# A decoder layer with experts: routed rows gathered in blocks, scores made by key, and an order planned in the source

## The chip, the cores and the metric

The kernel runs on one core of a Trainium2 chip. The metric is the device time of one execution in microseconds (us); the time of a kernel is the median over several runs. A profiled execution of each kernel gives the views that are quoted. The engines are PE (TensorE matmuls), PEld (its weight loads), DVE (VectorE), ACT (ScalarE), POOL (GpSimd) and SP (SyncE, which issues transfers here).

## The reference

One layer over 32 sequences of 128 tokens, width 128, 16 heads of width 8, all in fp32. Biases and gains are drawn at random, so none can be left out.

```
x, encoder_output: (32, 128, 128)     H, HD, FF, E, K = 16, 8, 512, 8, 2

def _attn(q_in, k_in, v_in, ..., causal):
    Q, Kp, V = q_in @ wq + bq, k_in @ wk + bk, v_in @ wv + bv      # by head
    scores = einsum('bqhd,bkhd->bhqk', Q, Kp) / sqrt(HD)           # -inf where causal and k > q
    a = softmax(scores)
    return einsum('bhqk,bkhd->bqhd', a, V) @ wo + bo

def _moe(x, ...):
    router_weights = softmax(x @ rw + rb)
    topw, topi = top_k(router_weights, 2);  topw = softmax(topw)
    combine[t, topi] += topw                                        # (tokens, 8)
    h = gelu(x @ w1[e] + b1[e]);  eo = h @ w2[e] + b2[e]            # every expert e
    return sum over e of eo[e] * combine[:, e]

x = layernorm(x + _attn(x, x, x, ..., True)) * g1 + b1
x = layernorm(x + _attn(x, encoder_output, encoder_output, ..., False)) * g2 + b2
x = layernorm(x + _moe(x)) * g3 + b3
```

## The kernel before, in words

Four sequences form a group (`G`), eight groups the input. The attention goes through groups: the loop at L409 runs the self attention of group `gi` and the cross attention of group `gi - 1` as two Python generators, one step of each in turn. There is no planner: each engine takes its instructions in the order in which the program writes them, and a tile pool makes an instruction wait until the buffer that it is to fill has been read.

In a group's attention, `transposed` (L200 to L205) turns the inputs on PE, ACT copies them out of PSUM. `keys_values` (L207 to L236) makes K under four head masks (`kb`) and V filled up with zeros to 32 columns a head. `probabilities` (L248 to L273) makes scores with a row for each query, eight heads at a time, in one of two PSUM pairs (`ps_sc`): where masked, first a bf16 product of the identity with the causal mask (L257), then two matmuls on tiles of 32 rows (L263). DVE takes each head's maximum (L268) and subtracts it (L269), and ACT takes the exponential (L272). `values` (L275 to L304) turns all 16 heads' probabilities on PE (L281), copies them out on ACT (L283), multiplies with V on column tiles of 128x32 (L285), turns the result back (L293) and divides it by its sum (L298, L299). Behind it come the output matmul (L320), the sum with the input (L322), and the norm: DVE's statistics (L174, L176), POOL's power (L177, L178), DVE's scaling (L180), POOL's gain and bias (L327, L328). `route` (L362 to L400) makes the router's logits, finds the two largest and leaves eight combine weights for each token, six of them zero.

The experts (L428 to L470) follow when all attention is done. For every group and every one of the eight experts, all 512 tokens go through: four matmuls of 512 columns (L448), four GELUs on ACT (L452), sixteen matmuls of 128 columns (L458), and four DVE steps that add the result times its combine weight (L463). Then the last norm and the store. Transfers: groups' inputs and results on SP's queue, experts' weights on POOL's (L404), all other weights on ACT's.

Of the kernel before, what the change touches and what calls it, by code (L numbers as in the profile page):

```python
# [9 lines left out]
BF16 = mybir.dt.bfloat16  # L10
U32 = mybir.dt.uint32
# [11 lines left out]
VC = 32  # columns of a column group of TensorE  # L23
RG = 4  # row groups of TensorE, of four heads each
EPS = 1e-05
SCALE = 1.0 / float(HD) ** 0.5
# Added to a masked score it leaves no bit of the score; exact in bfloat16.
MASKED = -(2.0**100)


def bc(ap, axis, n):
# [4 lines left out]
    return ap.broadcast_to(shape)  # L36


@with_exitstack
def kernel(  # L40
# [36 lines left out]
    NG = B // G  # L77

    const = ctx.enter_context(tc.tile_pool(name="const", bufs=1))
    keep = ctx.enter_context(tc.tile_pool(name="keep", bufs=1))  # L80

# [1 line left out]
    ident = const.tile([P, P], F32, name="ident")  # L83
    make_identity(nc, ident)
    ident16 = const.tile([P, P], BF16, name="ident16")
    nc.vector.tensor_copy(ident16, ident)

    # causal[q, r, k] = 0 where k <= q, else MASKED
    causal = const.tile([P, RG, P], BF16, name="causal")
    nc.gpsimd.memset(causal, 0.0)  # L90
    nc.gpsimd.affine_select(
        out=causal,
        in_=causal,
        pattern=[[0, RG], [-1, P]],
        compare_op=ALU.is_ge,
        fill=MASKED,
        base=0,
        channel_multiplier=1,
    )

    # hmask[p, r] = 1 where p lies in the head r of its row group: 0 <= p - 32 g - 8 r < 8 for a g
    hm4 = const.tile([P, RG, 4], F32, name="hm4")
    nc.gpsimd.memset(hm4, 1.0)
    nc.gpsimd.affine_select(
        out=hm4, in_=hm4, pattern=[[-32, RG], [-8, 4]], compare_op=ALU.is_ge,
        fill=0.0, base=0, channel_multiplier=1,
    )
    nc.gpsimd.affine_select(
# [59 lines left out]
    def normalize(y, name):  # L168
# [4 lines left out]
        for t in range(G):  # L173
            nc.vector.bn_stats(st[:, t, :], y[:, t, :])  # L174
# [337 lines left out]
```

## Time and profile before

| | before |
|---|---|
| median of 3 runs | 1370.74 us (1361.25 to 1379.28) |
| span of the profiled execution | 1358.0 us |
| PE busy | 1130.1 us (83%) |
| DVE busy | 549.3 us (40%) |
| ACT busy | 549.2 us (40%) |
| POOL busy | 146.6 us (11%) |
| attention, from the first to the last of its work on PE | 30.4 to 853 us |
| experts | 853 to 1347.5 us |

For the profiled execution the profile gives the span, from its first to its last record, and no time of its own beside it: the runs stand 3.25 to 21.28 us above that span. In the views, a group's row reads: line, engine, operation, out<-in, shapes, count, then busy us, mean ns of one, and the idle time ahead with what ended it. `128*32` is the tile of PE's array in use. A row of the windows reads: stretch, length, busy time and count for each engine, the clock granted to PE as a share of full speed, the share of time in which the DMA engines moved data, and GB/s.

### The profile page before, as it was taken

The page shows a single profiled execution, that of the slowest core. Times are in us where ns is not written, and L with a number is a line of the kernel's source. Part 1 is how long each engine was busy: PE and PEld are TensorE (multiplying, and loading weights), DVE is VectorE, ACT ScalarE, POOL GpSimd, SP SyncE. Part 2 cuts the span into 40 slices and gives each one's busy share as a digit, 9 for nine tenths or more (in the row PEclk, how much of TensorE's full clock was granted, in tenths as well). Part 3 has the DMA queues.
Part 4 walks back from the last instruction along what each step waited for, and adds up shares of the span by engine and source line. Part 5 has one row for each costly group of instructions (what it writes and reads, how often), then busy time and mean ns, then how long its engine had stood idle before and what let it go on. Part 6 is the DMA issues. An engine that isn't in the chain of part 4 may idle for free.

```text
span 1358.0 us, 17518 instructions
## 1 busy us (share of the span) xinstructions
PE 1130.1 (83%) x7196; PEld 697.2 (51%) x7233; DVE 549.3 (40%) x1286; ACT 549.2 (40%) x822; POOL 146.6 (11%) x173
## 2 busy tenths in 40 slices
PE   3969679579679858957957958799999999999996
PEld 1444344344344534543433433477777777776775
DVE  1548358266355356436636534222121221212121
ACT  1445345345343524524625623543333333343342
POOL 4020200300200020030030030101010110101011
PEclk9989879878975967778978975799999999999998
DMA  6000000000000000000000000000000000000000
GB/s 190 1 16 1 8 9 1 9 8 1 8 9 0 2 15 1 0 9 8 1 0 1 1 0 0 1 1 8 1 8 1 8 1 8 9 1 9 1 8 8
DMA packets 17551, 12.81 MB, mean 9 GB/s; under 512 B 1816, under 2 KB 16448, under 8 KB 17472
## 3 DMA queue, kind: packets, MB, share of 16 engines
q1 hardware_dynamic: 12672, 6.29, 1.6%
q0 software_dynamic: 1280, 4.20, 1.0%
q10 hardware_dynamic: 3520, 1.21, 0.4%
q8 instruction: 57, 0.93, 0.3%
q14 instruction: 22, 0.18, 0.0%
HBM read 9.60 MB, written 2.10 MB: 9 GB/s over the span
## 4 chain that ended last, share of the span: by engine, by line
PE 72%; DVE 12%; ACT 7%; POOL 4%; issue 3%; DMA 1%; ACTq 0%; POOLq 0%; DVEq 0%
PE po L458 17%; PE ph L448 17%; PE sc_s L263 7%; PE sc_c L263 5%; PE pt_c L281 5%; PE pt_s L281 4%; PE po_c L285 3%; PE po_s L285 3%; DVE nm_s L268 2%; DVE pr_s L269 2%; ACT prT_s L283 2%; PE pu_s L293 1%; POOL x L327 1%; POOL x L328 1%; PE sc_s L257 1%
## 5 line engine op out<-in xcount | busy, mean ns | idle before, releaser
L452 ACT ACTIVATE h<-ph,b1T 128x512 f32<-128x512 f32 x256 | 175.6, 687 | 291.2 <-PE ph L448 285.8
L458 PEld LDWEIGHTS po<-w,h 128*128 128x128 f32 x2048 | 247.9, 192 | 58.4 <-issue 43.5
L458 PE MATMUL po<-w,h 128*128 128x128 f32 x2048 | 250.1, 276 | 0.1
L448 PE MATMUL ph<-x2T,w 128*128 128x512 f32 x512 | 244.9, 600 | 0.0
L463 DVE SCALAR_TENSOR_TENSOR acc<-po,comb,acc 128x128 f32<-128x128 f32 x256 | 72.1, 344 | 359.2 <-PE po L458 359.2
L268 DVE TENSOR_REDUCE nm_s<-sc_s 128x8 f32<-128x1024 f32 x64 | 78.2, 1222 | 109.7 <-PE sc_s L263 109.7
L448 PEld LDWEIGHTS ph<-x2T,w 128*128 128x128 f32 x512 | 87.7, 192 | 62.3 <-issue 61.2
L263 PE MATMUL sc_s<-kb_s,q_s 32*128 32x512 f32 x256 | 107.7, 778 | 6.4 <-issue 2.3
L281 PE MATMUL pt_s<-ident,pr_s 128*128 128x128 f32 x512 | 87.8, 307 | 23.4 <-ACT pr_s L272 23.4
L268 DVE TENSOR_REDUCE nm_c<-sc_c 128x8 f32<-128x1024 f32 x64 | 77.9, 1217 | 60.9 <-PE sc_c L263 60.9
L283 ACT COPY prT_s<-pt_s 128x512 f32<-128x512 f32 x128 | 70.8, 586 | 69.8 <-PE pt_s L281 67.9
L283 ACT COPY prT_c<-pt_c 128x512 f32<-128x512 f32 x128 | 70.2, 588 | 69.1 <-PE pt_c L281 69.1
L272 ACT ACTIVATE pr_s<-pr_s 128x1024 f32<-128x1024 f32 x64 | 67.9, 1061 | 63.4 <-DVE pr_s L269 63.0
L281 PEld LDWEIGHTS pt_s<-ident,pr_s 128*128 128x128 f32 x512 | 62.0, 154 | 60.9 <-issue 34.6
L263 PE MATMUL sc_c<-kb_c,q_c 32*128 32x512 f32 x256 | 83.5, 764 | 8.2 <-DVE pr_s L269 4.8
L281 PE MATMUL pt_c<-ident,pr_c 128*128 128x128 f32 x512 | 88.5, 311 | 0.0
L272 ACT ACTIVATE pr_c<-pr_c 128x1024 f32<-128x1024 f32 x64 | 67.7, 1057 | 41.4 <-DVE pr_c L269 41.2
L204 PE MATMUL tp_x<-ident,x 128*128 128x128 f32 x64 | 16.1, 400 | 80.4 <-POOL x L328 78.5
L269 DVE TENSOR_TENSOR pr_c<-sc_c,nm_c 128x1024 f32<-128x1024 f32 x64 | 78.2, 1222 | 2.9
L269 DVE TENSOR_TENSOR pr_s<-sc_s,nm_s 128x1024 f32<-128x1024 f32 x64 | 77.6, 1212 | 1.0
L281 PEld LDWEIGHTS pt_c<-ident,pr_c 128*128 128x128 f32 x512 | 62.9, 156 | 28.9 <-issue 28.9
L285 PE MATMUL po_s<-prT_s,v_s 128*32 128x128 f32 x1024 | 56.1, 298 | 6.7 <-ACT prT_s L283 6.3
(140 smaller groups left out, 996.8 us busy)
## 6 DMA issues: line engine op xcount, KB each, us to landing
w<-in_L_xattn_e_w_dram POOLq DMA_DIRECT2D x16, 256.0 KB, 5.1
xg<-in_x_dram SPq DMA_DIRECT2D x8, 256.0 KB, 2.9
eg<-in_ctx_dram SPq DMA_DIRECT2D x8, 256.0 KB, 2.9
out_dram<-acc SPq DMA_DIRECT2D x8, 256.0 KB, 2.3
lng<-in_L_xattn_ln_g_dram ACTq DMA_DIRECT2D x3, 64.0 KB, 5.4
lnb<-in_L_xattn_ln_b_dram ACTq DMA_DIRECT2D x3, 64.0 KB, 4.5
wqs<-in_L_xattn_sa_wq_dram ACTq DMA_DIRECT2D x1, 64.0 KB, 3.4
wks<-in_L_xattn_sa_wk_dram ACTq DMA_DIRECT2D x1, 64.0 KB, 4.4
```

The lines of the kernel that those rows point to most:

```text
L204: nc.tensor.transpose(pt[:, b, :], src[:, b, :], ident)
L263: nc.tensor.matmul(sc[:, i], lhsT=q[rows, b, :], rhs=kb[rows, b], start=not masked, stop=True,)
L268: nc.vector.tensor_reduce(nm[:, hs], sc8, AX.X, ALU.max)
L269: nc.vector.tensor_tensor(pr[:, hs, :], sc8, bc(nm[:, hs], 2, P), ALU.subtract)
L272: nc.scalar.activation(pr[:, hs, :], pr[:, hs, :], AF.Exp, scale=SCALE)
L281: nc.tensor.transpose(pt[:, r, :], pr[:, 4 * g + r, :], ident)
L283: nc.scalar.copy(prT, pt)
L285: nc.tensor.matmul(po[VC * r : VC * r + VC, g, :], lhsT=v[:, b, 4 * g + r, :], rhs=prT[:, r, :], start=True, stop=True,)
L448: nc.tensor.matmul(ph, lhsT=w1[:, e, c * P : (c + 1) * P], rhs=x2T[:, bs, :], start=True, stop=True,)
L452: nc.scalar.activation(h[:, c], ph, AF.Gelu, bias=b1T[:, e * NFC + c : e * NFC + c + 1])
L458: nc.tensor.matmul(po[:, b, :], lhsT=h[:, c, b, :], rhs=w2[:, e, c, :], start=c == 0, stop=c == NFC - 1,)
L463: nc.vector.scalar_tensor_tensor(acc[:, b, :], po[:, b, :], comb[:, G * gi + b, e : e + 1], acc[:, b, :], ALU.mult, ALU.add,)
```

## The change

The whole body is written anew; the computation stays. Five things are different.

**Order.** Each piece of work is a task with an engine, a duration, a priority and the buffers that it fills or reads. `Plan.run` goes through them with a clock of its own and those durations: an engine that is free takes the ready task of the lowest priority number for which slots are free. `Plan.emit` then writes the instructions in that order. PSUM is three pairs (`sc0` to `sc2`) and two single banks (`mm0`, `mm1`).

**Scores twice.** For each tile (a sequence, or parts of two in the self attention, where the causal half that is masked is mostly left out) scores are made by query on tiles of 32x64, and DVE takes only their maxima. POOL splits a maximum into two bf16 parts, PE turns them. Three tiles later the scores are made again by key, with bf16 matmuls (`sel`) that subtract the query's maximum in PSUM, and ACT takes the exponential straight from PSUM. The probabilities then lie by key, as the values need them. The head masks lie on the queries (`qm`), which four SP transfers from SBUF to SBUF spread out for each group and attention.

**Values.** Two heads share a window of 32 columns; the turning back and the division are done with DVE's transposes of 32x32.

**Routing.** The place of each token in its expert's region is counted by a triangular matmul; eight indirect POOL transfers a group write the rows to `rows_d` in DRAM, and eight more fill up the regions' last blocks.

**Experts.** 71 blocks of 128 rows. A small table made from the counts gives each block its expert and its first row; 17 blocks use rows of the first four groups alone. SP loads the table's entry into a register and the block's rows from DRAM, DVE loads an entry too and copies the expert's 1156 columns of weights and biases, and the block's result goes to `res_d` by an indirect POOL transfer. `final` loads two results for each token, weighs and adds them.

```
-    for gi in range(NG):                         # experts: every group x every expert
-        for e in range(E):
-            for c in range(NFC):
-                nc.tensor.matmul(ph, lhsT=w1[:, e, c * P : (c + 1) * P], rhs=x2T[:, bs, :], ...)
-                nc.scalar.activation(h[:, c], ph, AF.Gelu, bias=b1T[:, e * NFC + c : ...])
...
+    NL = 3
+    for i in range(NT + NL):
+        sq = sq_tiles[i] if i < NT else None
+        sk = sk_tiles[i - NL] if i >= NL else None
...
+        for h in range(2):
+            qp = Buf(pairs) if sq is not None else None
+            kp = Buf(pairs) if sk is not None else None
...
+            t = pe(step_time(sq, sk), i + 0.5 * h - AHEAD,
+                lambda ...: emit_step(sq, h, qp, sk, kp), deps, bufs, "32x64")
+            if sq is not None:
+                ms.append(maximum(sq, h, qp, nm, i + 0.5 * h + 0.1 - AHEAD, t))
+            if sk is not None:
+                te = add("ACT", act(1024), i + 0.5 * h + 0.1 - AHEAD,
+                    lambda ...: nc.scalar.activation(
+                        prb.at[:, 8 * kh : 8 * kh + 8, :]..., kp.at..., AF.Exp, scale=SCALE), [t], [kp, prb])
...
+    def emit_step(sq, h, qpair, sk, kpair):
+        kh = 1 - h                                # row groups 2 * kh + i for sk, 2 * h + i for sq
+        if sk is not None: ...                    # 4 matmuls, a sequence's keys x 4 heads of queries
+                        mm(o[:, :, c0 : c0 + nq], it.k.at[rr, s, k0 : k0 + HALF], qs, n == 0, False)
+        if sq is not None: ...                    # 16 matmuls, 64 queries of a head x 128 keys
+                            mm(o, q_, it.k.at[rr, s, k0 : k0 + nk], r == 0 and n == 0, ...)
...
+        if sk is not None: ...                    # 16 bf16 matmuls
+                    mm(o, sel[rr, r, :], nm_, False, r == 3)
...
+        def masked():                             # queries(): under queries' head masks
+            for r in range(4):
+                nc.sync.dma_start(out=it.qm.at[r::4, r, :], in_=it.q.at[r::4, :])
...
+    def block(s):
+        def ld():
+            r = nc.sync.value_load(tab_r[0:1, s : s + 1], ...)
+            ins = nc.sync.dma_start(out=xr_(), in_=rows_d[bass.ds(r, P), :])
...
+        def wcopy():
+            r = nc.vector.value_load(tab_w[0:1, s : s + 1], ...)
+            nc.vector.tensor_copy(w.at...[:, 0:WB], flat[:, bass.ds(r, WB)])
...
+        t = pe(0.14, pr0 - 1.5, lambda: nc.tensor.transpose(bt.at[:, 0:P], xr_()[:, 0:P], ident), ...)
+        t = add("ACT", act(P), pr0 - 1.4, lambda: nc.scalar.copy(xT.at[:, 0:P], bt.at[:, 0:P]), ...)
...
+        t = pe(0.95, pr0, gemm1, [t, t_w, last_step], [xT, w, pp])
+        t = add("ACT", 4 * act(P, 1), pr0 + 0.5, gelu, [t, *exps_all], [pp, w, h])
+        t = pe(0.95, pr0 + 1.5, gemm2, [t], [h, w, pp])
+        t = add("DVE", 0.55, pr0 + 2, result, [t], [pp, w, xr, o, idb])
+        t_res.append(add("POOL", 1.2, pr0 + 2.2, scatter, [t], [o, idb], lat=2.2))
...
+    plan.run()
+    plan.emit()
```

The planned order shows best on the engines. PE before, in the middle of the attention: the self attention of group 4 (`s4`) and the cross attention of group 3 (`c3`) in turn, scores (`sc`), values (`po`), turned results (`pu`) and turned probabilities (`pt`), each in a buffer of its own name.

```order
L263 MATMUL sc_c3_0_0_2907<-kb_c3_2873,q_c3_2900 128x512 x2
L263 MATMUL sc_c3_0_1_2913<-kb_c3_2873,q_c3_2900 128x512 x2
L285 MATMUL po_s4_0_2951<-prT_s4_0_2_2979,v_s4_2829 32x128 x3
L285 MATMUL po_s4_0_2951<-prT_s4_0_3_2990,v_s4_2829 32x128 x4
L257 LDWEIGHTS ident16_66
L257 MATMUL sc_s4_1_0_2921<-causal_68,ident16_66 128x512
...
L263 MATMUL sc_s4_1_0_2921<-kb_s4_2822,q_s4_2841 128x512 x2
L293 MATMUL pu_s4_0_2998<-ident_61,uT_s4_0_2996 128x128 x3
...
L281 MATMUL pt_c3_0_0_3007<-ident_61,pr_c3_0_2905 128x128 x2
```

PE after, in the middle of the attention: a projection, one half-step (key scores from `qm2` and `k2` into `sc0`, query scores into `sc1`, maxima `nmT2` into `sc0`), a piece of values (`pr`, `v1`), and the start of the next half-step.

```order
L597 MATMUL mm1_69<-xT1_124,wkcp_113 128x512
L702 MATMUL sc0_65<-qm2_132,k2_135 64x512 x4
L702 MATMUL sc1_66<-k2_135,qm2_132 64x128 x16
L702 LDWEIGHTS sel_75
L702 MATMUL sc0_65<-nmT2_148,sel_75 64x128
...
L702 MATMUL mm0_68<-pr4_153,v1_137 32x128 x4
L702 MATMUL mm1_69<-pr4_153,v1_137 32x128 x4
L702 MATMUL mm0_68<-pr1_150,v1_137 32x64 x4
...
L702 MATMUL sc0_65<-qm2_132,k2_135 64x512 x4
L702 MATMUL sc2_67<-k2_135,qm2_132 64x128 x16
```

The turned probabilities are gone; key scores of one half-step and of the next go into the same slot, query scores alternate between two, and one other piece of work stands between half-steps. All small matmuls go through the helper `mm` at L702.

DVE before, in the experts: results (`po`) of one group's experts, added one after the other, with the norm of the group before among them.

```order
L463 SCALAR_TENSOR_TENSOR acc_4_7481<-po_4_7_7746,comb_146,acc_4_7481 128x128 x4
L174 BN_STATS st_m4_7767<-acc_4_7481 128x6 x4
L176 BN_AGGR mv_m4_7768<-st_m4_7767 128x2 x4
L437 COPY combT_5_7793<-pc_5_7788 8x512
L180 TENSOR_SCALAR acc_4_7481<-acc_4_7481,mv_m4_7768,rs_m4_7769 128x128 x4
L443 TENSOR_TENSOR acc_5_7787<-pb2_5_7795,x2_144 128x512
L463 SCALAR_TENSOR_TENSOR acc_5_7787<-po_5_0_7814,comb_146,acc_5_7787 128x128 x4
```

DVE after, in the experts: row numbers (`id`) and result (`o`) of a block, then the load of a register from the table (`tab_w`), and the copy of a later block's weights from `wall` into one of the three slots `qm`.

```order
L1489 TENSOR_SCALAR id0_225<-xin1_122,tab_e_202 128x1
L1492 TENSOR_TENSOR o0_221<-sc0_65,qm1_131 128x128
L1449 TENSOR_LOAD tab_w_204
L1449 ISA x2
L1450 ISA
L1450 COPY qm1_131<-wall_89 128x1156
L1489 TENSOR_SCALAR id1_226<-xT1_124,tab_e_202 128x1
L1492 TENSOR_TENSOR o1_222<-sc1_66,qm2_132 128x128
```

Result, register load and copy now take turns on DVE, and the copy fills the slot of the weights that the result just read has used.

More of the change, by code (lines that the diff above doesn't have):

```diff
@@ L5 @@
 from concourse import mybir
-from concourse.masks import make_identity
 from concourse._compat import with_exitstack
@@ new lines, with transposes, fn @@
+    NT = len(sq_tiles)
+    first = {}
+    for i, (kind, gi, _) in enumerate(sq_tiles):
+        first.setdefault((kind, gi), i)
+    class Item:
+        pass
+    items = {}
+    before = {}
+    def transposes(src, prio, deps, bufs, halves=False):
+        bank = Buf(singles)
+        def fn():
+            for i in range(G):
+                o = bank.at[:, i * P : (i + 1) * P]
+                if halves:
+                    o = bank.at.rearrange("p (a h k t) -> p a k h t", a=2, h=2, k=2)[:, i // 2, i % 2]
+                nc.tensor.transpose(o, src()[:, i, :], ident)
+        return bank, pe(0.5, prio, fn, [*deps, t_ident], [bank, *bufs])
@@ new lines, with wait_for @@
+    s_m16 = Slots(places(2, [P, 64], "m16", BF16))
+    exps_all = []
+    kept, every = [], []
+    sync = mybir.DependencyInfo(mybir.DependencyClass.Sync, mybir.DependencyReason.DATA)
+    behind = set()
+    def wait_for(ins, group, needed):
+        tc.declare_no_dep(ins.ins, group=group, keep=list(needed), reason="other rows")
+        for w in needed:
+            if w.name not in behind:
+                behind.add(w.name)
+                tc.add_manual_dep(ins.ins, w.name, sync, reason="rows it reads")
@@ new lines, in rows_written @@
+    def rows_written(ins, gi=None):
+        tc.declare_no_dep(ins.ins, group="rows", reason="rows of their own")
+        tc.declare_no_dep(ins.ins, group="loads", reason="loads of blocks read other rows")
+        tc.add_to_no_dep_group("rows", ins.ins)
+        every.append(ins.ins)
+        if gi is not None and gi <= GF:
+            kept.append(ins.ins)
+    turns = [("s", 0)]
+    for gi in range(NG):
+        if gi + 1 < NG:
+            turns.append(("s", gi + 1))
+        turns.append(("c", gi))
@@ new lines, in table, with look @@
+        t = add("DVE", 2.2, dve_prio + 0.02, ranks, [t, t_misc], [b3_, cb])
+        if which == "first":
+            cnt_f["inf"] = t
+        def look():
+            for v_ in range(2):
+                for h in range(2):
+                    nc.tensor.matmul(
+                        b4_.at[:, NS * v_ : NS * v_ + nS], lhsT=evals[:, h, v_ : v_ + 1].broadcast_to([P, P]),
+                        rhs=hot[:, h, :], start=h == 0, stop=h == 1,
+                    )
+        t = pe(0.6, prio + 0.03, look, [t, t_blk], [b4_])
@@ new lines, in result, with scatter @@
+        def result():
+            nc.vector.tensor_scalar(
+                idb.at, xr_()[:, P + 1 : P + 2], tab_e[:, s : s + 1], xr_()[:, P : P + 1], ALU.is_lt, ALU.add
+            )
+            nc.vector.tensor_tensor(o.at, pp.at[:, 1, 0:P], wv()[:, 2 * FF + NFC : WB], ALU.add)
+        t = add("DVE", 0.55, pr0 + 2, result, [t], [pp, w, xr, o, idb])
+        def scatter():
+            ins = nc.gpsimd.indirect_dma_start(
+                out=res_d[:, :], out_offset=bass.IndirectOffsetOnAxis(ap=idb.at[:, 0:1], axis=0),
+                in_=o.at, in_offset=None, bounds_check=2 * B * P - 1, oob_is_err=False,
+            )
+            tc.declare_no_dep(ins.ins, group="res", reason="results of their own")
+            tc.declare_no_dep(ins.ins, group="resloads", reason="loads of sums read other results")
+            tc.add_to_no_dep_group("res", ins.ins)
+            res_ins.append((s, ins.ins))
```

1443 lines of the change are left out of this document (1117 added, 326 removed).

## The prediction

> **What bounds the kernel now.** I read the page's head first, then the chain of waits by engine, then a table of windows, one for each stage.
>
> ```profile
> span 1358.0 us, 17518 instructions
> PE 1130.1 (83%) x7196; PEld 697.2 (51%) x7233; DVE 549.3 (40%) x1286; ACT 549.2 (40%) x822; POOL 146.6 (11%) x173
> PE 72%; DVE 12%; ACT 7%; POOL 4%; issue 3%; DMA 1%; ACTq 0%; POOLq 0%; DVEq 0%
> ...
> 0.00:30.40 30.40, 9.08 (x21) 4.29 (x21) 4.15 (x12) 4.08 (x5) 16.78 (x34) 1.00 0.66 184
> 30.40:853.00 822.60, 636.48 (x4367) 345.17 (x4404) 437.66 (x860) 355.53 (x543) 95.68 (x103) 0.82 0.02 6
> 853.00:1347.50 494.50, 484.57 (x2808) 347.75 (x2808) 104.72 (x402) 189.56 (x276) 30.37 (x32) 0.99 0.02 5
> 1347.50:1358.00 10.50, 0.00 (x0) 0.00 (x0) 2.76 (x15) 0.00 (x0) 3.79 (x4) 0.61 0.09 25
> ```
>
> TensorE carries 72% of the chain. The windows (length, busy time of PE, PEld, DVE, ACT and POOL, granted clock, DMA share, GB/s) give 30 us of start, 823 us of attention at clock 0.82, 495 us of experts in which PE is 98% busy, and a tail of 10.5 us. The low clock has a place:
>
> ```profile
> 404.50:441.90 37.40, 36.69 (x127) 15.65 (x128) 21.54 (x22) 13.95 (x19) 0.00 (x0) 0.50 0.00 1
> 442.00:472.00 30.00, 27.98 (x289) 15.65 (x289) 11.79 (x18) 17.55 (x30) 1.44 (x2) 1.00 0.01 1
> 404.50:441.90 37.40, 20.91 (x33) 5.17 (x32) 0.50 0.00 1
> 442.00:472.00 30.00, 12.47 (x80) 8.44 (x80) 1.00 0.01 1
> ```
>
> The third row is the score matmuls (L263) alone, the fourth the transposes (L281) alone. At half clock PE is busy 98% of the time, most of it with tiles of 32 rows; at full clock it is busy 93%, most with tiles of 128x128. The Trainium skill ("TensorE: Matmul & The Clock Gate", Part 1) says that the gate watches how busy PE is; by that alone 98% would not run at half clock, so here the trace disagrees: how much of the array works decides too.
>
> **The change part by part.** The prices come from these groups (busy us, mean ns of one) and stretches (start, us):
>
> ```profile
> L458 PE MATMUL po<-w,h 128*128 128x128 f32 x2048 | 250.1, 276 | 0.1
> L448 PE MATMUL ph<-x2T,w 128*128 128x512 f32 x512 | 244.9, 600 | 0.0
> L281 PE MATMUL pt_s<-ident,pr_s 128*128 128x128 f32 x512 | 87.8, 307 | 23.4 <-ACT pr_s L272 23.4
> L257 PE MATMUL sc_s<-causal,ident 128*128 128x512 bf16 x91 | 35.7, 446 | 21.9 <-DVE pr_c L269 16.7 <-POOL iota_i L118 2.6 <-DVE pr_s L269 2.6
> L268 DVE TENSOR_REDUCE nm_s<-sc_s 128x8 f32<-128x1024 f32 x64 | 78.2, 1222 | 109.7 <-PE sc_s L263 109.7
> L272 ACT ACTIVATE pr_s<-pr_s 128x1024 f32<-128x1024 f32 x64 | 67.9, 1061 | 63.4 <-DVE pr_s L269 63.0
> L205 ACT COPY xT<-tp_x 128x512 f32<-128x512 f32 x8 | 4.7, 586 | 4.8 <-PE tp_x L204 4.5
> L404 POOL DMA_DIRECT2D w<-in_L_xattn_e_w_dram x8 | 6.1, 757 | 0.0
> L322 DVE TENSOR_TENSOR y_s<-py_s,xg 128x512 f32<-128x512 f32 x8 | 5.5, 692 | 14.5 <-PE py_s L320 14.5
> ...
> 514.48 0.84 PE L285 MATMUL po_s<-prT_s,v_s 128*32 128x128 f32 x18
> 515.33 1.14 PE L263 MATMUL sc_c<-kb_c,q_c 32*128 32x512 f32 x8
> 562.49 1.13 PE L263 MATMUL sc_s<-kb_s,q_s 32*128 32x512 f32 x4
> 563.67 1.22 DVE L268 TENSOR_REDUCE nm_s<-sc_s 128x8 f32<-128x1024 f32 x1 [3.74 <-PE sc_s L263]
> ...
> xg<-in_x_dram SPq DMA_DIRECT2D x8, 256.0 KB, 2.9
> ```
>
> *Attention.* Gone are the 1024 transposes of probabilities, their copies on ACT and the subtraction on DVE. Scores are now made twice, by query for the maxima and by key for the exponentials, in 118 half-steps (59 tiles, two halves each). The order shows what paces them: key scores always lie in the slot sc0, so the next half-step's first matmul waits until the last half-step's exponential has read it. PE and ACT therefore take turns, and the other work of PE has to stand in the holes. Behind the waiting matmul stand the query scores and, behind those, DVE's maximum, which has three tiles of lead.
>
> One half-step on PE: four key matmuls of 512 columns on four tiles. L263 does four such matmuls (eight records) on four row groups in 1.14 us. The 16 query matmuls of 128 columns lie on the other two row groups, four to a tile, thus the same 512 columns beside them: nothing more if the eight tiles run at once, another 1.14 if they do not. No run here shows tiles half as wide and as tall at once; I take the first, since four tiles do overlap in both rows of 128x32 and of 32x128 tiles. Then 16 bf16 matmuls that subtract the maximum, 512 columns a tile: at most L257's 0.446, at least 0.24, a quarter of an fp32 matmul of L448 (244.9/256 = 0.957); I take 0.25, since most of L257's stand at half clock. That is 1.39, 1.4 with the causal masks of some. Then the exponential, 1.06 by L272, and two hand-overs of 0.05 (562.49 + 1.13 = 563.62, and DVE starts at 563.67): 1.4 + 1.06 + 0.1 = 2.56 us. 118 x 2.56 = 302 us.
>
> DVE's maximum is 1.22 in that pitch and does not pace it. While ACT works, PE has a hole of 2.56 - 1.4 = 1.16 us. The rest of a group has to stand there: four transposes of 4 x 0.171 (87.8/512), four projections of 0.957, five sets of four 128-column matmuls at 0.244 (250.1/1024) and eight pieces of values of 16 matmuls on column tiles, of which L285 does nine in 0.84, so some 1.1 each. That is 2.7 + 3.8 + 4.9 + 8.8 = 20, 21 with the small ones. Most pieces fit a hole. Once a group the order puts some ten, 7.2 us, between two half-steps, 6.0 more than the hole; three long ones elsewhere add 0.5 each: 7.5 x 8 groups = 60, taken as 61. Attention: 302 + 61 = 363 us. As a check, PE alone would need 118 x 1.4 + 8 x 21 = 333, DVE 112 x 1.22 plus about 17 a group = 273. The ends: 300 if PE's own steps overlap better and nothing falls between; 363 + 118 x 1.14 = 498 if query and key matmuls do not overlap.
>
> The masked queries now come by four transfers on SP's queue, about 2.9 us behind the projection (xg's row); they are issued some five tiles ahead (25 us), so I cost them at nothing, and at 2.9 x 16 = 46 us without that cover.
>
> The 64 scatters of rows, 0.757 to issue (L404), add 48 us to POOL's 95.68 within 363: covered. The last group's eight feed only blocks behind the first 17.
>
> *Experts.* Before, every expert sees every group: 64 units at 494.5/64 = 7.73 us. Now 71 blocks of 128 rows run, however the rows fall. Rows for the rest:
>
> ```profile
> L452 ACT ACTIVATE h<-ph,b1T 128x512 f32<-128x512 f32 x256 | 175.6, 687 | 291.2 <-PE ph L448 285.8 <-POOL x L327 4.5
> L375 ACT ACTIVATE lg<-lg 128x32 f32<-128x32 f32 x8 | 1.8, 229 | 18.5 <-DVE lg L374 18.5
> L463 DVE SCALAR_TENSOR_TENSOR acc<-po,comb,acc 128x128 f32<-128x128 f32 x256 | 72.1, 344 | 359.2 <-PE po L458 359.2
> L174 DVE BATCH_NORM_STATS2 st_s<-y_s 128x6 f32<-128x128 f32 x32 | 7.0, 280 | 0.3
> L176 DVE BATCH_NORM_AGGREGATE mv_s<-st_s 128x2 f32<-128x6 f32 x32 | 2.9, 152 | 0.0
> L452 ACT ACT_TABLE_LOAD x3 | 3.8, 1283 | 1.4 <-PE py_c L320 1.4
> w<-in_L_xattn_e_w_dram POOLq DMA_DIRECT2D x16, 256.0 KB, 5.1
> ```
>
> PE, per block: eight matmuls at 0.244 and a transpose at 0.171: 2.12. ACT: GELU of 128 columns is 0.687 less 384 x 0.84 ns (the slope from L375's 32 columns to L272's 1024, (1061 - 229)/992) = 0.365, four of them, 0.26 for the copy, 0.2 for a share of the norms: 1.9. DVE: the block's weights are copied by one instruction of 1156 columns; by the nearest row, L268's 1024 columns at 1.222, in 1.38. The result takes 0.16 + 0.29, the last sums 8 x (8 x 0.344 + 4 x 0.28 + 4 x 0.152 + 0.16) = 37 us, 0.52 a block. 2.35 in all, a little over PE's 2.12, and the register load ahead of the copy comes on top. Nothing of before shows one; from nothing up to the 1.283 of the only load row, the table load, and I take it small, since a block has three slots of weights and the wait is for few bytes. Experts: 71 x 2.35 = 167 us; 151 if PE sets the pace, 258 with the load at 1.283.
>
> The Trainium skill ("VectorE: DVE Perf Modes", Mode 2x_2P) has fp32 copies from SBUF to SBUF at two elements a cycle; by that the copy were near 0.7, DVE below PE, and the experts 151. No run here shows such a copy.
>
> *Between and behind.* The first GELU waits for every exponential, and ACT's copies for later blocks are queued behind it, so behind the last score come values, norm, logits and routing of the last group: about 25 dependent steps between 0.15 and 1.04, L322's 0.69 and L205's 0.59 among them, plus the table load: 17 us. At the end the last block's scatter lands (5.1), its sums are read (2.9), and before's tail of 10.5 follows: 18. The start stays at 30, since it is loads of the same weights; -8 to +5.
>
> Sum: 30 + 363 + 17 + 167 + 18 = 595 us of span against 1358. The runs stand 3.25 to 21.28 above the span, the median 12.7: **608 us**.
>
> **The rivals.**
>
> ```profile
> 514.47:514.75 0.28, 0.28 (x13) 0.27 (x16) 0.00 (x0) 0.16 (x1) 0.00 (x0) 1.00 0.00 0
> 775.70:785.70 10.00, 9.35 (x118) 5.75 (x120) 1.10 (x4) 5.70 (x11) 1.44 (x2) 1.00 0.01 2
> ```
>
> *PE starved of instructions.* A half-step holds 112 (four for an fp32 matmul, two for bf16). Over ten busy microseconds before issues 238, 42 ns each; its best stretch 29 in 0.28 us, 9.7 ns. At 9.7 a half-step needs 1.09, hidden; from 12.5 on it paces. At 20 ns, between the rows, 2.24: +0.84 x 118 = 99, and by the same count some 45 for the values: about 750. The Trainium skill ("Runtime: NRT & Kernel Launch", Instruction fetch mechanics) speaks of a floor of some 20 cycles an instruction; at the 1.2 GHz that its page "TensorE: Matmul & The Clock Gate" (Part 1) gives the sequencer that were 16.7 ns, and about 700 us. The stretch at 9.7 ns lies below it, so for PE the trace disagrees. Chance 0.10.
>
> *DVE paces the experts.* Register load 1.283 and copy 1.38 in one queue: 3.63 a block, 71 x 1.28 = 91 more: about 700. For it: the block's order has result, load and copy on DVE in turn. Against it: the load could run while DVE's last work drains. Chance 0.12.
>
> *Half clock in attention.* All tiles are small, and PE stands still during the exponential. PE's 1.4 becomes 2.8, other work doubles: +1.4 x 118 + 40: about 810. By the skill's rule on how busy PE is, those pauses would speak for it. Against it: key and query tiles of a half-step use all four row groups at once, where a half of L263 uses two, and from 442 to 472 PE stayed at 1.00 on mixed work with gaps. Chance 0.06.
>
> *Tighter.* Holes take all, PE sets 300 in attention and 151 in experts, and 5 us less goes into the start: 25 + 300 + 17 + 151 + 18 + 12.7 = 524, 510 to 540. Chance 0.08.
>
> *Slower: the indirect scatter.* Each block ends in one on POOL, one row a descriptor, and DVE's copies may hold it up. With 595 - 167 = 428 elsewhere it makes the kernel no faster once a block takes (1358 - 428)/71 = 13.1 us, and 13.5 gives about 1400. The nearest rows are 0.757 to issue and 5.1 to land a contiguous load, and four result slots overlap them: far away. The Trainium skill ("SBUF — State Buffer", Who interferes with whom) has two-port copies of DVE lock out POOL's descriptor writing for an instruction's length; even 1.38 on 0.757 stays under a block's 2.35. Chance 0.03, of which 0.01 ends within 2%.
>
> **How the numbers follow.** The forecast, from 540 to 690 by the holes, the tiles' overlap and the register load each somewhere between its ends, has 0.61. 510 takes in the tight case, 755 the cases of DVE and of instructions; half clock and slower stay out with the edges: 510 to 755. A measurement of this kernel can tell about 2%, 27 us. Only the scatter reaches there, so faster 0.97, same 0.01, slower 0.02.
>
> **What would show it.** Attention of some 363 us with the next half-step's first key matmul waiting for ACT's exponential; the sum is wrong if that wait is gone or if DVE ends it. PE's granted clock near 1.0 there. A key part of 1.4 us; 2.5 means that the tiles do not overlap. In the experts 2.1 to 2.4 us a block; DVE's copy at 1.38 or 0.7, and idle time ahead of it tells the register load. POOL idle between scatters. The prediction fails as a whole if a transfer (masked queries, rows) ends most of PE's idle time.

## The result and the profile after

The kernel after takes 828.66 us (median of 4 runs, 823.59 to 835.05) against 1375.01 us: 0.604 of the time, 95% interval 0.600 to 0.609. The forecast was 608 us with a range up to 755. Its sign was right and its size was not. Executions of one kernel spread by up to 5% with the granted clock, so medians are compared, and where single runs come close to each other the ranges or the fastest runs stand beside them.

The head and the chain of waits of the page after; the profiled execution took 831.82 us:

```profile
span 829.9 us, 29414 instructions
PE 627.8 (76%) x12628; PEld 492.9 (59%) x12628; DVE 402.7 (49%) x1077; ACT 309.6 (37%) x717; POOL 301.4 (36%) x455
PE 45%; issue 13%; ACT 12%; POOL 10%; DMA 9%; DVE 7%; SPq 2%; ACTq 1%; POOLq 0%; DVEq 0%
```

PE's share of the chain fell from 72% to 45%; ACT, POOL, transfers and bare issue now hold a tenth each. The windows of the kernel after by stage (columns as before: length, busy time of PE, PEld, DVE, ACT and POOL, granted clock, DMA share, GB/s), cut at the first query scores, the first key scores, the end of the last exponential, the first GELU and the last block:

```profile
0.00:26.65 26.65, 9.27 (x36) 7.08 (x36) 11.51 (x37) 4.73 (x7) 12.57 (x34) 1.00 0.33 69
26.65:52.18 25.53, 16.30 (x332) 12.70 (x331) 9.98 (x25) 3.45 (x7) 1.61 (x8) 0.64 0.78 232
52.18:568.50 516.32, 423.70 (x10925) 309.44 (x10928) 240.65 (x568) 189.42 (x302) 141.82 (x266) 0.83 0.07 22
568.50:588.00 19.50, 11.98 (x148) 9.98 (x139) 16.05 (x80) 7.76 (x21) 11.87 (x18) 0.79 0.02 8
588.00:808.00 220.00, 166.50 (x1198) 153.74 (x1198) 120.21 (x351) 102.57 (x379) 128.20 (x125) 0.86 0.26 71
808.00:829.90 21.90, 0.00 (x0) 0.00 (x0) 4.32 (x18) 1.65 (x4) 5.34 (x6) 0.59 0.16 48
```

| stage | forecast | measured | difference |
|---|---|---|---|
| start | 30 | 26.65 | -3 |
| attention | 363 | 541.9 | +179 |
| between | 17 | 19.5 | +2.5 |
| experts | 167 | 220.0 | +53 |
| end | 18 | 21.9 | +4 |
| beside the span | 12.7 | 1.9 | -11 |

Two stages hold the error.

**Attention.** The groups of instructions (of the two score groups the first named is by key, the second by query) and PE's longest waits in the attention:

```profile
L1222 ACT ACTIVATE pr<-sc 128x1024 f32<-128x1024 f32 x112 | 114.5, 1024 | 241.3 <-PE sc L702 197.3
L702 PE MATMUL sc<-qm,k 32*64 32x512 f32 (+1 forms) x1024 | 149.1, 666 | 46.8 <-ACT pr L1222 44.8
L702 PE MATMUL sc<-k,qm 32*64 32x128 f32 (+1 forms) x4096 | 195.8, 303 | 9.8 <-DMA qm<-q 4.6
```

```profile
PE sc L702 <- ACT pr L1222: 44.8, 57, 1.3
...
PE mm L702 <- issue: 7.7, 8, 1.6
PE sc L702 <- issue: 7.5, 9, 1.8
...
PE sc L702 <- DMA qm<-q: 4.6, 10, 1.8
```

The serial chain is the one that the forecast named: key matmuls wait for the exponential, 57 times, and it for them. I took each half-step's parts from the records: from the first key matmul to the end of the last `sel` matmul (the PE part); from there to the exponential; the exponential; and from its end to the next key matmul. They add up to 251 + 22 + 110 + 130 = 514 us. Of 108 half-steps (four more can't be told apart in the records), 64 have a PE part of 1.73 us on average (1.4 forecast) and 44 a long one, over 2 us and 3.2 on average. Of the long ones, 30 ran at half clock, which here means a mean granted clock under 0.75 in the PE part. The other 14 ran at full clock: four of them hold waits of PE for masked queries, eight hold pauses in which PE waits for nothing that the profile shows ("issue"). Here are PE's rows where a stretch of half clock begins (start, us) and windows around it:

```profile
290.75 1.09 PE L702 MATMUL sc<-qm,k 32*64 32x512 f32 x8
292.54 1.04 PE L702 MATMUL sc<-k,qm 32*64 32x128 f32 x16 [0.70 <-DMA qm<-q]
...
296.00 0.34 PE L702 MATMUL sc<-k,qm 32*64 32x128 f32 x4 [1.81 <-DMA qm<-q]
```

```profile
234.00:255.00 21.00, 16.34 (x481) 12.22 (x479) 11.65 (x35) 11.52 (x21) 8.97 (x19) 1.00 0.10 32
...
280.00:292.00 12.00, 10.48 (x135) 6.77 (x119) 6.73 (x23) 6.33 (x12) 4.67 (x8) 1.00 0.14 42
292.00:300.00 8.00, 5.17 (x101) 3.50 (x108) 1.39 (x2) 3.75 (x7) 3.21 (x3) 0.78 0.17 60
300.00:320.00 20.00, 17.06 (x317) 12.99 (x316) 9.70 (x34) 5.76 (x9) 6.39 (x16) 0.50 0.05 16
```

PE pauses for masked queries, the clock falls, and from 300 to 320 it stays at 0.50 although PE is busy 85% of the time. From 234 to 255 the same kind of work runs at 1.00 and 78% busy. At half clock the same work keeps PE busy for longer (four of the records of key matmuls 1.13 us from 297.88 on, 0.66 from 234.18 on), so these two shares alone don't tell what sets the clock.

The "issue" pauses come 17 times, 15.2 us in all, 7.5 ahead of scores and 7.7 ahead of values. One and the next are 256 records of PE (matmuls and weight loads together) or a multiple of 256 apart, give or take one. Each ends 1.2 to 1.6 us after a packet of the instruction queue has landed; that queue moved 99 packets of 16 KB, 1.62 MB in all (packets, MB, share of 16 engines):

```profile
q8 instruction: 99, 1.62, 0.8%
```

So PE seems to run out of instructions at these places. This is read from the trace; no run tested it.

Of the 130 us between exponential and next key matmul, eight gaps at the turn of a group hold 96.5 (21.2, 8.1, 9.6, 8.3, 8.5, 15.8, 6.7, 18.4), 28 short ones 31.5. Pieces of the longest ones on PE:

```profile
92.22 1.63 PE L590 MATMUL mm<-ident,y 128*128 128x128 f32 x4 [4.68 <-ACT y L939]
...
422.31 1.54 PE L1373 MATMUL mm<-hot_first,evals 128*128 128x17 f32 x8 [0.67 <-ACT xT L621]
...
526.54 1.63 PE L590 MATMUL mm<-ident,y 128*128 128x128 f32 x4 [3.68 <-ACT y L939]
```

The first and the last group's cross attention has to wait for its self attention's whole tail (values, norm, projection), and no half-step is placed in between. In the gap of 15.8 the table for the first 17 blocks (L1324 to L1373) stands in the order as well.

**Experts.** Results follow each other every 1.9, 1.9, 1.6 and 3.2 us in the undisturbed stretch, 2.15 on average. The other blocks lose time in two ways. The first, with the waits from 588 to 808 and rows of POOL and DVE:

```profile
PE sc L1463 <- DVE qm L1450: 35.8, 13, 12.7
...
DVE id L1489 <- DMA res_d<-o,id: 17.5, 2, 16.2
```

```profile
606.54 1.22 POOL L1103 DMA_INDIRECT rows_d<-x,rid  x1 [0.30 <-issue]
...
619.55 0.97 POOL L1418 DMA_INDIRECT rows_d<-fillrow,fid  x1 [0.30 <-issue]
620.83 0.97 POOL L1497 DMA_INDIRECT res_d<-o,id  x1 [0.30 <-issue]
...
623.11 0.27 DVE L1489 TENSOR_SCALAR id<-xin,tab_e 128x1 int32<-128x1 f32 x1 [16.18 <-DMA res_d<-o,id]
...
684.46 0.77 DVE L1450 COPY qm<-wall 128x1156 f32 x1 [0.37 <-DVE o L1492]
687.79 0.35 DVE L1529 SCALAR_TENSOR_TENSOR y<-pr,wlo,x 128x128 f32<-128x128 f32 x1 [2.57 <-DMA pr<-res_d]
...
692.18 0.28 DVE L1492 TENSOR_TENSOR o<-sc,qm 128x128 f32<-128x128 f32 x1
```

The last group's scatters and the fills, one every 1.27 us, stand in POOL's queue ahead of the blocks' results. The four result slots fill up, and DVE waits 16.18 us. The second way: `final` puts eight sums and the statistics, 4.2 us in one piece, into DVE's queue, and ahead of them DVE waits for a load of `res_d` (2.57 us here). So no block's result starts between 683.81 and 692.18, and later groups do the same at 708, 737, 768 and 793.

### The profile page after: what moved, and what is told of

It reads as the page before. It is cut to its first block, busy times and chain, and to the rows that moved or that the text cites. A ratio compares the mean times of both kernels' runs of the same rounds, so it can differ in the third digit from the quotient of the medians.

```text
span 829.9 us, 29414 instructions
## 1 busy us (share of the span) xinstructions
PE 627.8 (76%) x12628; PEld 492.9 (59%) x12628; DVE 402.7 (49%) x1077; ACT 309.6 (37%) x717; POOL 301.4 (36%) x455
## 3 DMA queue, kind: packets, MB, share of 16 engines
q8 instruction: 99, 1.62, 0.8%
## 4 chain that ended last, share of the span: by engine, by line
PE 45%; issue 13%; ACT 12%; POOL 10%; DMA 9%; DVE 7%; SPq 2%; ACTq 1%; POOLq 0%; DVEq 0%
PE sc L702 27%; ACT pr L1222 9%; PE mm L702 7%; POOL res_d L1497 5%; DMA pr<-res_d 3%; PE mm L597 2%; DMA res_d<-o,id 2%; PE mm L590 2%; PE mm L643 1%; POOL rows_d L1103 1%; DMA qm<-q 1%; DVE y L1532 1%; PE mm L960 1%; PE mm L600 1%; ACT y L939 1%
## 5 line engine op out<-in xcount | busy, mean ns | idle before, releaser
L791 DVE TENSOR_REDUCE nm<-sc 128x8 f32<-128x1024 f32 (+1 forms) x112 | 136.9, 1224 | 220.4 <-PE sc L702 219.9
L1222 ACT ACTIVATE pr<-sc 128x1024 f32<-128x1024 f32 x112 | 114.5, 1024 | 241.3 <-PE sc L702 197.3
L702 PE MATMUL sc<-k,qm 32*64 32x128 f32 (+1 forms) x4096 | 195.8, 303 | 9.8 <-DMA qm<-q 4.6
L702 PE MATMUL sc<-qm,k 32*64 32x512 f32 (+1 forms) x1024 | 149.1, 666 | 46.8 <-ACT pr L1222 44.8
L702 PEld LDWEIGHTS sc<-k,qm 32*64 32x64 f32 x4096 | 146.6, 154 | 49.0 <-issue 34.6
L1463 PE MATMUL sc<-q,qm 128*128 128x128 f32 x568 | 88.0, 310 | 38.4 <-DVE qm L1450 35.8
L1471 ACT ACTIVATE k<-sc,qm 128x128 f32<-128x128 f32 x284 | 80.8, 373 | 84.2 <-PE sc L1463 74.4
L1463 PEld LDWEIGHTS sc<-q,qm 128*128 128x128 f32 x568 | 80.1, 221 | 43.1 <-DVE qm L1450 33.6
L1497 POOL DMA_INDIRECT res_d<-o,id x71 | 77.0, 1085 | 51.8 <-DVE o L1492 42.0
L1480 PE MATMUL sc<-qm,k 128*128 128x128 f32 x568 | 82.1, 291 | 16.2 <-ACT k L1471 15.3
L702 PE MATMUL mm<-pr,v 64*32 64x128 f32 (+2 forms) x3072 | 74.8, 276 | 14.3 <-issue 7.7
L702 PEld LDWEIGHTS sc<-qm,k 32*64 32x64 f32 x1024 | 32.3, 151 | 75.8 <-ACT pr L1222 65.9
L702 PEld LDWEIGHTS mm<-pr,v 64*32 64x32 f32 (+1 forms) x3072 | 59.6, 114 | 25.4 <-issue 14.3
L702 PE MATMUL sc<-nmT,sel 32*64 32x128 bf16 x1792 | 54.3, 241 | 1.1 <-issue 1.1
L702 PEld LDWEIGHTS <-sel 32*64 32x64 bf16 x1792 | 41.8, 120 | 8.6 <-issue 7.3
L882 DVE STREAM_TRANSPOSE u<-mm 128x512 f32<-128x512 f32 x32 | 21.9, 703 | 30.5 <-PE mm L702 30.4
```

The source lines that it names most:

```text
L702: nc.tensor.matmul(out_, lhsT=lhsT, rhs=rhs, start=start, stop=stop, skip_group_check=True)
L791: lambda: nc.vector.tensor_reduce(dst(), src(), AX.X, ALU.max, negate=True), [dep], [pair, nm],
L882: t = add("DVE", dve(512), prio, lambda: nc.vector.transpose(u1.at, bank.at), [dep], [bank, u1])
L1222: lambda kp=kp, prb=prb, kh=kh: nc.scalar.activation(prb.at[:, 8 * kh : 8 * kh + 8, :].rearrange("p h q -> p (h q)"), kp.at.rearrange("p b ...
L1463: nc.tensor.matmul(pp.at[:, 0, c * P : (c + 1) * P], lhsT=wv()[:, c * P : (c + 1) * P], rhs=xT.at[:, 0:P], start=True, stop=True)
L1471: nc.scalar.activation(h.at[:, c, :], pp.at[:, 0, c * P : (c + 1) * P], AF.Gelu, bias=wv()[:, 2 * FF + c : 2 * FF + c + 1],)
```

## The experiments

Kernels on one chip are compared with each other. The last exponential marks the end of attention.

**PE's half-step: masks and `sel` ahead of the query scores.** The records show that key and query tiles do run at once, but the `sel` matmuls that finish the key scores stand behind the query matmuls.

```
     def emit_step(sq, h, qpair, sk, kpair):
         if sk is not None: ...     # 4 key matmuls
+        if sk is not None: ...     # masks and 16 sel matmuls
         if sq is not None: ...     # 16 query matmuls
-        if sk is not None: ...     # masks and 16 sel matmuls
```

> Edit: in each half-step the masks and the 16 bf16 matmuls that finish the key scores are written ahead of the 16 query matmuls. In the trace of the changed kernel a half-step at full clock takes 1.65 to 1.9 us on PE until the exponential may start, and the pitch is 2.9 to 3.1 us. Theory: the finishing matmuls stand behind the query matmuls in PE's queue, so the turn of PE and ACT is longer than the key part alone. Then the PE part falls to about 1.3 us and the pitch to 2.5: 0.45 x 112 = 50 us less, some 70 with the half-clock steps; 760 to 785 us. Rival: PE's total work sets the pace, and the query matmuls only push other work out of the holes. Then less than 15 us change: 815 to 830 us.

919.86 us (ratio 0.671, 0.664 to 0.678), against 867.25 for e4 on the same chip, which leaves the attention's order as it was (below). That lies outside both expected ranges. The PE part at full clock is 1.43 us against 1.76 in e4, so the query matmuls ahead of `sel` cost the difference. But the time from exponential to next key matmul is 225 us against 129: the query matmuls, now behind `sel`, run in the next half-step's way. Attention as a window of this kernel:

```profile
52.00:660.70 608.70, 562.02 (x10930) 369.07 (x10932) 241.15 (x569) 194.23 (x302) 142.01 (x266) 0.69 0.06 19
```

PE is 92% busy at clock 0.69. At such a clock PE's own total is a bound too, close behind the serial chain.

**Clock: more work for PE, on large or small tiles.** In e2 two full bf16 matmuls of 512 columns follow each half-step; in e3 they use 32x32 of the array.

```
+                def fill(b=qnext):
+                    for _ in range(2):
+                        mm(b.at[0:128, 0]..., ones16[0:128, 0:128], bc(ones16[0:128], 1, 4), True, True)
+                pe(0.45, i + 0.5 * h + 0.05 - AHEAD, fill, [t, t_misc0], [qnext])
```

> Edit: two bf16 matmuls of 512 columns on the whole 128x128 array, with results that are overwritten, into the next half-step's query slot, in the hole behind each half-step. Theory: the granted clock falls to 0.5 after a pause because small tiles use too little of the array, and stays there; 44 of 109 half-steps ran so, 3.42 us of PE part against 1.92. Then the clock in the attention rises from 0.82 to 0.97 or more, and the time falls by up to 44 x 1.5 = 66 us less some 10 to 20 for crowded holes: 765 to 800 us. Rival: the clock has another cause than PE's work, or pauses alone (waits for the masked queries) set it. Then it stays near 0.82 and the time at 829 or up to 40 us more.

> Edit: as the run with the whole array, but the two extra matmuls use a tile of 32 rows and 32 columns, a sixteenth of the array, for the same time. Theory that the used area decides: clock near 0.82, 829 to 860 us. Rival that PE's busy time decides: the same gain as with the whole array, clock 0.97 or more and 765 to 800 us.

870.86 (867.74 to 873.1) and 898.47 us (895.27 to 918.63), at clocks of 0.87 and 0.83. The tile alone is worth 28 us. With full tiles the kernel comes out at e4's time: 15 half-steps at half clock (25 with small tiles, 34 in e4), but the filling stands in the chain, and the gaps grow from 129 to 145 us.

**Sums later, first way.** The planner counts 3 us from a group's last scatter to its loads; here 9.

```
-        t = add("SP", 0.2, pr0, ld, [*t_res[: s + 1], *exps_all], [r], lat=3.0)
+        t = add("SP", 0.2, pr0, ld, [*t_res[: s + 1], *exps_all], [r], lat=9.0)
```

> Edit: one number; the plan counts 9 us instead of 3 for the loads of the results that the sums wait for, so the sums and norms of a group stand some three blocks later in DVE's order. In the trace of the changed kernel blocks come every 1.6 to 3.2 us, 2.15 in the mean, but seven times 6.4 to 13.5 us pass between two results, with DVE idle until the load of results has landed (scatter 2.4, load 4.5 us). Theory: DVE's queue stands still for that wait, and the weights of the next blocks behind it. Then about 45 us of the 220 in the experts go: 775 to 795 us. Rival: the blocks are held by the loads of their rows or by POOL's scatters, which wait no less: 820 to 830 us.

867.25 us, and from the first to the last result 214 us, where the kernel after takes 216: hardly a gain. The sums moved, but two groups' sums then stand together. The four kernels so far ran on one chip, where ACT and DVE were also late seven to nine times an execution, 34 us in all, in a way that the kernel after doesn't show. I come back to that below; because of it these four are compared with each other only.

**The kernel after again, and three edits beside it,** on another chip without those waits.

> The changed kernel itself, unedited, beside the next three on the same chip. In the four runs before this one ACT and DVE waited seven to nine times for 2 to 7 us for a signal from PE while POOL scattered a group's rows, which the first profile of the changed kernel does not show. If these waits come from the edits, this run is again 824 to 835 us without them; if they come from the chip or the moment of the run, it shows them too and takes 850 to 870 us.

838.02 us, but from 819.2 at a mean clock of 0.855 to 846.0 at 0.815: the spread of its runs goes with the clock. In the profiled execution 44 half-steps ran at half clock, not 30.

Sums at low priority, spread among the blocks by the planner:

```
-        pr0 = X0 + s + 3
+        pr0 = X0 + NS + 20 + 4 * gi
```

> Edit: the sums, norms and stores of all eight groups get a priority behind the last block, so no work of theirs stands between blocks. Theory: in the experts the 6.4 to 13.5 us between some results are these lumps of a group (load awaited, eight sums, statistics, about 8 us on DVE in one piece), against three slots of weights. Then blocks run at 2.15 us throughout except for the stall near the start, from the first GELU to the last block's second product 71 x 2.15 + 15 = 168 us instead of 220, and the end grows from 22 to about 60: 810 to 825 us in all beside 829. Rival: POOL's scatters or the loads of rows hold the blocks: then the long pauses stay, the first-to-last time is above 200 us, and the whole time 850 to 870 us.

807.84 us (791.9 to 816.36), 30 less by the medians and 27 by the fastest runs. First to last result takes 196 us instead of 216 (213 in the unedited run on this chip), and the lumps above 8 us are gone. The pause of 17.5 stays. The end hardly grows: 25 us from the last result, 22 in the kernel after. So some 17 to 20 of the 30 us belong to the sums. The attention of the profiled execution is 25 us shorter too, at a clock of 0.85 against 0.78, which the edit does not explain.

Masked queries planned for with a longer transfer:

```
-        ... add("SP", 0.3, prio + 0.2, masked, [t, *t_qz], [it.q, it.qm], lat=2.5)
+        ... add("SP", 0.3, prio + 0.2, masked, [t, *t_qz], [it.q, it.qm], lat=5.0)
```

> Edit: one number; the plan counts 5.0 us instead of 2.5 for the four transfers that spread the masked queries. In the trace they take 3.5 us to land behind 1.8 us of issue, and in two of seven groups PE stands still for them for 2 to 3 us, after which the clock is 0.57 to 0.62 for the next 28 to 36 us. Theory: that pause starts the half-clock stretches. Then the order has other work there, half-clock half-steps fall from 44 to some 25, and the time by 20 to 35 us: 795 to 810. Rival: the half clock comes with the small tiles whatever precedes them: 825 to 835 us.

863.51 us, slower. PE's waits for `qm` went from 4.6 to 0.7 us, its weight loads' from 12.6 to 4.9, yet 36 half-steps were still at half clock, some in stretches without such a wait. So that wait is one occasion of the half clock and not its only cause. The gaps at the groups' turns grew to 122 us, and the first exponential comes at 67 us instead of 52.

Fill rows written by plain transfers at the start, without the eight indirect fills:

```
+    for e in range(E):                      # eight ACT-queue transfers of fillrow over the regions
+        t_dummy = add("ACTQ", 0.12, 6 + 0.01 * e, lambda e=e: prefilled(e), ...)
-    for e in range(E):                      # eight indirect POOL transfers
-        t_fill.append(add("POOL", 1.2, X0 - 1.5 + 0.01 * e, fill, [t_fid], lat=2.2))
```

> Edit: the eight indirect transfers of POOL that fill up the regions' last blocks behind the last group are left out; instead all of the region is filled at the start by eight plain transfers of 2.2 MB each on ACT's queue. Theory: the 17.4 us between two results near the start of the experts are POOL's queue, where 16 indirect transfers of about 1.2 us stand ahead of the blocks' own scatters. Then that pause falls to about 8 us: 9 to 10 us less, 815 to 825 us. Rival: the blocks there wait for the table or for rows to land, not for POOL's queue: no change beyond 3 us. Against the gain: 17.6 MB more move in the first 100 to 150 us, and the transfers of masked queries may wait behind them, up to 20 us more.

The pause fell from 17.5 to 7.2 us, which puts it on POOL's queue. The whole is slower, 885.13 us: the first exponential comes at 92 us instead of 52, behind the transfers.

**Filling only PE's idle places,** on top of the sums at low priority: up to two single matmuls a half-step, with a priority behind all other work; e9 on the full array, e12 on 32x32 in the same order.

```
+            for n_ in range(2):
+                fb = Buf(singles)
+                def fill(fb=fb):
+                    mm(fb.at[0:128]..., ones16[0:128, 0:128], bc(ones16[0:128], 1, 4), True, True)
+                pe(0.25, 500 + i + 0.5 * h, fill, [t, t_misc0], [fb])
```

> Edit: the sums behind the last block in priority, as in the run that did this alone, and 236 bf16 matmuls of 512 columns on the whole array, written into a single PSUM bank that is free, at the lowest priority: the plan puts them only where PE would stand still, two for each half-step on average. Theory: half clock comes from too little of the array in use and holds itself; full-array work in the idle places lifts it. Then half-clock half-steps fall from 42 to 56 in the runs without it to under 20, without the crowding that fixed places brought: 30 x 1.45 = 43 us less than 808 of the run with late sums alone: 760 to 780 us. Rival: the extra work delays what is critical by as much as the clock gives: 795 to 815 us.

> Edit: the same order, instruction for instruction, but the 236 extra matmuls use a tile of 32x32, a sixteenth of the array. Theory that the used area decides: about as many half-clock half-steps as without extra work (40 or more), 25 to 50 us slower than with the whole array. Rival that PE's busy time decides: the same time within 8 us and as few half-clock half-steps.

776.56 us (771.07 to 778.48) and 809.54 us (784.87 to 821.05), against 807.84 without filling. The full tiles leave 7 of 108 half-steps at half clock (29 without filling) and a mean clock of 0.92 to 0.93 in each run. With small tiles one execution, the profiled one, did nearly as well (784.87, clock 0.914, 9 half-steps), the others did not (0.864 to 0.887). By the fastest runs the tile is worth 14 us here, by the medians 33, so this pair alone doesn't show it. That called for another test.

**Sixteen result slots instead of four,** with the sums late and no result ahead of the last group's routing, and then all three edits together.

```
-    s_o = Slots(places(4, [P, P], "o"))
+    s_o = Slots(places(4, [P, P], "o") + [12 slices of v_t])
```

> Edit: the sums behind the last block in priority, and sixteen instead of four slots for the blocks' results and row numbers (the values' tiles of the attention are reused). Theory: near the start of the experts the blocks stand still for 17.5 us because four results fill their slots while POOL issues 16 transfers of rows at 1.27 us. With sixteen slots the pause falls to under 5 us: 12 to 15 us less than with late sums alone, 790 to 797 us. Rival: the pause is the wait for rows of the last group, which no slot can shorten: 805 to 810 us.

> Edit: late sums, sixteen result slots and the full-array extra work together. If the two causes are separate places, the gains add: 12 to 15 us below the run with extra work and four slots; 745 to 768 us.

791.59 and 763.44 us (ratio 0.560, 0.554 to 0.565). The longest step between two results is 6 us in both. PE's wait for the blocks' weights in the kernel with the slots alone:

```profile
PE sc L1464 <- DVE qm L1451: 19.8, 19, 3.9
```

The 12.7 us at once are gone. The three edits together beat the kernel after on the same chip by 75 us (63 by the fastest runs).

**The area of the array, once more:** the last kernel with filling on 128x128, on 128 rows x 32 columns, and on 32x32, five rounds on a third chip.

```
-                    mm(fb.at[0:128]..., ones16[0:128, 0:128], bc(ones16[0:128], 1, 4), True, True)
+                    mm(fb.at[0:32]..., ones16[0:128, 0:32], bc(ones16[0:128], 1, 4), True, True)   # e14
+                    mm(fb.at[0:32]..., ones16[0:32, 0:32], bc(ones16[0:32], 1, 4), True, True)     # e13
```

> The sums at the end, sixteen result slots, and in each half-step up to two bf16 matmuls of 512 columns that fill PE's idle places on all 128 rows and 128 columns of the array; on one chip with the two kernels that differ from it in the size of those matmuls alone. Both theories expect some 763 us and a mean granted clock of 0.93 to 0.95.

> The same order with the filling matmuls on 128 rows and 32 columns. If the clock follows the area of the array in use, it lies between the other two: some 775 us and a clock near 0.90. If only PE's busy time counts, it is the full tile's time, 763 us within 1%. If rows count and columns don't, also 763.

> The same order with the filling matmuls on 32 rows and 32 columns. Area theory: some 790 us, the time without any filling (791.59), at a clock of 0.86 to 0.89. Busy theory: 763 us within 1%, at 0.93 to 0.95.

835.07 (0.610, 0.606 to 0.613), 840.82 (0.616, 0.612 to 0.619) and 863.82 us (0.632, 0.627 to 0.637). The number of instructions and their order are the same, so PE's busy share alone does not decide: the small tile costs 29 us on this chip by the medians (25 by the fastest runs, and the ranges, 827.33 to 841.24 and 852.3 to 879.6, do not meet). The mean clock is 0.884 to 0.903 with the full tile and 0.830 to 0.859 with the small one. Matmuls on all rows but a quarter of the columns give 23 of the 29; whether columns count at all stays open, since the intervals of the first two touch and their fastest runs differ by 0.9 us.

The same kernel took 763.44 us on one chip and 835.07 on this one. These are the waits of e15 whose releaser the profile calls remote, and rows of one of them:

```profile
ACT pr L1229 <- remote: 61.1, 9, 8.8
...
DVE nm L791 <- remote: 26.8, 5, 6.7
```

```profile
174.49 0.37 PE L702 MATMUL sc<-nmT,sel 32*64 32x128 bf16 x11 [0.30 <-issue]
...
177.32 0.97 POOL L1103 DMA_INDIRECT rows_d<-x,rid  x1 [0.30 <-issue]
...
179.03 1.02 ACT L1229 ACTIVATE pr<-sc 128x1024 f32<-128x1024 f32 x1 [6.94 <-remote]
```

PE has finished the scores by 175, and ACT starts at 179, 0.7 us behind the last of four scatters on POOL. Nine such waits add 36 us to the exponentials' start; others stand in the experts. Such waits stand in all seven traces from two of the chips and in none of the other nine, the kernel after's among them. What delays the signal, and why only there, was not settled.

## Why the prediction was wrong, and where it was right

**What held.** The rival of DVE did not occur, and that of instructions only in part. DVE's copy took 0.76 us in the undisturbed stretch, 0.82 on average, not the 1.38 of L268's row. The estimate of near 0.7, worked out from the two elements a cycle of the Trainium skill ("VectorE: DVE Perf Modes", Mode 2x_2P), was the closer one, as the row shows:

```profile
L1450 DVE COPY qm<-wall 128x1156 f32 x71 | 58.2, 821 | 29.4 <-DVE o L1492 22.8
L1497 POOL DMA_INDIRECT res_d<-o,id x71 | 77.0, 1085 | 51.8 <-DVE o L1492 42.0
```

The load of a register adds some 0.5 us, seen as idle time ahead of the copy. Together they leave DVE below the pitch, and the 2.15 us of an undisturbed block is PE's 2.12: PE is 96% busy there. A scatter issues in 1.09, far from the 13.1 of the slower rival. PE passed the 112 instructions of a half-step in 1.58 us at best, 14.1 ns each. That is under the floor of 16.7 ns, an estimate from the Trainium skill ("Runtime: NRT & Kernel Launch", Instruction fetch mechanics). So the slower rate that this rival feared did not come; instead PE paused 17 times, 15.2 us in all, where its next instructions seem to have been missing. The forecast had no term for that.

**Attention, 363 forecast, 541.9 measured.** Three terms were mis-sized, and the first of them had left out two kinds of stop.

- "118 x 2.56 = 302". The PE part with its hand-over was to take 1.45; 112 of them 162 us. It took 251 + 22 = 273. Some 66 of the 111 us are the 44 long half-steps, 3.42 with their wait instead of 1.93. About 43 of these 66 belong to the 30 at half clock, about 22 to the 14 at full clock with their waits for masked queries and pauses. The forecast had half clock as a rival at 0.06 for the whole attention; it came for about a third of the time (mean clock 0.83). The reason against it there, that all four row groups work and that PE stayed at 1.00 on mixed work with gaps, was not enough. The other 45 us are the short part in every half-step. "Nothing more if the eight tiles run at once" fails by 0.3 us although they do run at once: the first experiment shows 1.43 without the query matmuls ahead of `sel`, 1.73 with them.
- "6.0 more than the hole", once a group. The usual gap is 8 to 10, and the first, sixth and eighth are 21.2, 15.8 and 18.4. With the exponentials 185 us were forecast and 240 measured. That those three gaps come from a group's dependent chain and from the block table is read from the trace; no run took it away, so the cause of these 55 us is argued and not shown.
- The six half-steps ahead of the first key scores took 25.5 us, 10 more than at the forecast's pitch, at a clock of 0.64 and with the DMA engines 78% busy.

The masked queries, "issued some five tiles ahead (25 us), so I cost them at nothing", failed at the groups' starts. The direct wait is small; what follows it, from 300 to 320 us for one, is half clock for 20 us and more, and that is not. Why the clock stays low there was not settled. The Trainium skill ("TensorE: Matmul & The Clock Gate", Part 1) looks at how busy PE is. Here PE was 85% busy at 0.50 and 78% busy at 1.00, and on one chip filling with the same number of matmuls gave a clock of 0.884 to 0.903 with large tiles and of 0.830 to 0.859 with small ones. The measurement decides: how much of the array the filling uses counts too; by what measure stays open.

**Experts, 167 forecast, 220 measured.** The 71 x 2.35 counted engine times. It named result slots ("four result slots overlap them") for the scatter's landing, but not the 16 other scatters ahead of them in POOL's queue: a pause of 17.5 us, some 15 beyond the pitch, removed by more slots. And it spread the last sums evenly, 0.52 a block, where they stand in DVE's in-order queue in one piece, behind a load that is not there yet. Moving them took 17 to 20 us off the time from the first to the last result. With both edits that time is 180 us (e10), still more than 71 x 2.15 = 153; what holds the rest was not tested.

**The rest** is small: start -3, between +2.5, end +4, and 11 us less beside the span than before's median had.

The range ended at 755 because each bound was taken by itself. Half clock for a part, longer gaps and stalls in the experts came together.

## What to carry to other kernels

A sum of engine times is a floor. Where a list schedule sets in-order queues, look for what stands ahead of a critical instruction in its own queue, with measured latencies, and count the slots that cover it. And where all tiles are small and PE takes turns with another engine, price the half clock for a part of the time rather than as an all-or-nothing rival; a few large matmuls in idle places can be worth more than they cost.

## What was not expected of the hardware

A clock of 0.50 lasts while PE is 85% busy with small tiles. One kernel, unchanged, gave 763 and 835 us on two chips, while the kernel before differed by 0.2% (1367.8 and 1370.4); 36 us of it are starts of ACT that come only after a row of indirect transfers on POOL, and PE's parts of the half-steps add 19, with more of them at half clock (11 against 4). And in the kernel after PE stood still for 15.2 us, with nothing to wait for in the profile, in 17 places that lie 256 of its records or a multiple apart. A ratio between two kernels of this kind holds for the chip on which it was taken.
